# A state-space scan kernel: who carries the wait for a buffer's former sums, and when the second chunk's conv rows may start

## The chip, the cores and the metric

One core of one Trainium2 chip runs the whole program in one launch. Its engines are PE (TensorE: matmul; PEld is its weight load), DVE (VectorE), ACT (ScalarE), POOL (GpSimd) and SP (SyncE, which issues the DMAs here). Each has its own stream of instructions, in order; they meet through semaphores. The metric is the device time in microseconds (us); the time before is 6586.43, the median of three runs (6583.84 to 6587.49).

## The reference

Four layers on an image tensor of 4 x 96 x 64 x 64, fp32. Layer 0 is a selective scan in four directions with an MLP behind it, layer 1 a smaller scan, layer 2 a Fourier mixer and a quantized MLP, layer 3 a linear attention and a quantized MLP. The change touches layer 0 alone. Cut to what matters:

```python
# b = 4 images, L = 64*64, 192 inner channels d, 16 states n, 4 directions k
xz = t_ln @ in_proj_w.T + in_proj_b
xi, z = split(xz)
xi = silu(depthwise_conv_3x3(xi) + conv_b)
xs = the pixels of xi by rows, by columns, and both reversed      # [b, k, d, L]
x_dbl = einsum('bkdl,kcd->bkcl', xs, x_proj_w)                    # dts_r (6), Bs (16), Cs (16)
dt = softplus(einsum('bkrl,kdr->bkdl', dts_r, dt_projs_w) + dt_projs_b)
for each l:
    h = h * exp(dt[l] * A) + dt[l] * B[l] * x[l]                  # h: [b, k, d, n]
    y[l] = sum over n of h * C[l]
y = y + Ds * xs, the four directions are summed
out = (layernorm(y) * silu(z)) @ out_proj_w.T
```

## The kernel before, in words

**Steps and units.** The scan of layer 0 is cut into 64 steps: 4 images b, 4 directions k (in the order 0, 1, 3, 2), 4 chunks of 1024 pixels. A step has 24 units, 1536 in all. A unit is a tile of 128 partitions (32 channels x 4 states) by 1024 pixels; its index i is made of j (3 groups of channels), q (4 groups of states) and p (2 halves of the group), in the order j, q, p.

**One unit** goes through five coroutines:
- `sources` (L1498): POOL writes w = u * bb, with u = dt * x and bb = B loaded so that rows are repeated. The tile w comes from a ring of six buffers (`WB = 6`, L1356), so unit i takes the buffer of unit i - 6.
- `decays` (L1477): ACT writes h = exp(dt * A) into one of two PSUM tiles. The turn of decay i begins when the product of unit i - 2 is done; first a column of the old h is copied into `state`, which the same unit of the next chunk starts from.
- `recurs` (L1509): DVE runs the scan in place in h, with h and w as inputs; then, as its next instruction, the C product: w = h * cc, over the same w. A scan waits for ACT's h and POOL's w.
- `side` (L1535): for every twelfth unit the scan writes w, and POOL forms the product; 128 units go this way.
- `gathers` (L1544): PE adds the products of two units over the states with the matrix sel4 into the PSUM tile py, 32 rows at a time; `collects` (L1601) has ACT copy py to the sum Y.

**Waits.** The semaphores are set by the framework, which tracks who has read and written each tile. POOL's writing of w in unit i waits for PE's sums of unit i - 6, the last readers of that buffer. The C product writes the same tile, and in the program before most of these products wait for those sums on PE as well, besides the scan just ahead on DVE. [...]

**Chunks.** `preludes` (L1374) prepares a step: it loads xi, forms the 38 columns of x_proj on PE, stores B and C, forms delta (PE; Abs, Relu, Exp, Ln on ACT; an addition and a multiplication by x on POOL) and stores delta and delta * x to a DRAM tile dd. `loads_du` and `loads_bc` bring u, dt, bb and cc back with rows repeated. For the first step delta is formed in three pieces; when the last of them has its Ln, the event "begun" (L1422) is posted.

**The front of image 0.** `front(0)` (L456) normalizes and projects the image, then runs the 3 x 3 conv in 12 row blocks of 8 image rows: `conv(part, q)` (L560). Part 0 has 128 of the channels with q from 0 to 7; part 1 has the other 64, two halves of the image at once, with q from 0 to 3. A block is nine matmuls with diagonal weights into a PSUM bank (`bm`), or, if it is `early` (L568), nine multiply-adds on DVE (`taps`, L404); then Silu on ACT, a store to xi_d by SP, and a transposing copy to xt on POOL. Chunk 0 needs the blocks (0,0), (0,1), (1,0), (1,1); chunk 1 needs (0,2), (0,3), (1,2), (1,3). The blocks in `order` run ahead of the scan; the others, `rest_` (L613), in two workers beside it. [...]a Silu in the scan phase has a table load on each side. When all blocks are through, SP stores the transposed image for the directions 1 and 3.

**What sets the order.** The coroutines are driven by `Work` (L111 on), which keeps an estimated time for each engine and always advances the coroutine whose next instruction could start first (`choose`, L162). So the order on each engine is fixed when the program is built. A wait on an event such as "begun" holds a coroutine back in this planning; on the chip there are only the engines' streams and the semaphores. The layers behind the scan run as further coroutines (`others`, L1625) between the units, and for the last image after them.

Of the kernel before, what the change touches and what calls it, by code (L numbers as in the profile page):

```python
# [13 lines left out]
ALU = mybir.AluOpType  # L14
# [31 lines left out]
def size(x):  # L46
    return x.free_size() if hasattr(x, "free_size") else x[:].free_size()


def on(engine, *events, banks=0, took=0.7, table=None, unit=None):  # L50


    return engine, events, banks, took, table, unit
# [9 lines left out]
class Work:  # L63
# [40 lines left out]
    def post(self, *key, stored=False):  # L104
        self.events[key] = self.me.stored if stored else self.me.end
# [25 lines left out]
    def drop(self, *tiles):  # L131
        for t in tiles:
            self.free[self.held.pop(id(t))] = self.me.end
# [83 lines left out]
def tile_hybrid(ctx: ExitStack, tc: tile.TileContext, I: dict, out: bass.AP):  # L217
# [5 lines left out]
    def mm(o, lhsT, rhs, **kw):  # L223
        n = size(o)
        each = 0.97e-3 if rhs.dtype == E5M2 else 0.93e-3 if size(lhsT) <= 64 else 1.9e-3
        wk_.spend("pe", max(n * each, 0.3 if n > 4 else 0.2) + 0.02, 0.3)
        return nc.tensor.matmul(o, lhsT=lhsT, rhs=rhs, **kw)  # L227
# [5 lines left out]
    def act(o, i, func, **kw):  # L233

        want = TABLES.get(func, func if func in OTHER else None)
        if want is not None and want != wk_.table:
            wk_.spend("act", 1.28)
            if func in TABLES:
                nc.scalar.preload_act_table_set(want)
            wk_.table = want  # L240
        wk_.spend("act", 0.2 + size(o) * 0.87e-3)
        return nc.scalar.activation(o, i, func, **kw)  # L242
# [25 lines left out]
    ve, po_ = Side(nc.vector, "dve", on_vector), Side(nc.gpsimd, "pool", on_pool)  # L268
# [37 lines left out]
    def load_const(name, shape, src=None):  # L306
        t = const.tile(shape, F32, name=name)
        nc.sync.dma_start(t, I[src or name])
        return t
# [5 lines left out]
    sel4 = load_const("sel4", [128, 32])  # L315
# [7 lines left out]
    def V(name, rows=128, j=0, n=1):  # L323
        c, w = _COL[name]
        assert j + n <= w
        return vec[0:rows, c + j : c + j + n]
# [77 lines left out]
    def taps(acc, xp, row, w):  # L404

        o = acc.rearrange("p (h w) -> p h w", w=WW)
        for k in range(9):
            kh, kw = divmod(k, 3)
            v = xp[:, row + kh : row + kh + 8, kw : kw + 64]
            if k % 3 == 0:  # L410
                yield on("dve")
            if k == 0:
                ve.tensor_scalar(o, v, w[:, 0:1], None, ALU.mult)
            else:
                ve.scalar_tensor_tensor(o, v, w[:, k : k + 1], o, ALU.mult, ALU.add)
# [9 lines left out]
    def wt(pool, rows, name, t, cols=HC, dt=F32):  # L425
        name = f"{name}_{t}"
        return pool.tile([rows, cols] if isinstance(cols, int) else [rows, *cols], dt, tag=name, name=name)
# [28 lines left out]
    def front(b):  # L456
# [4 lines left out]
        ahead_ = b == 0  # L461
# [98 lines left out]
        def conv(part, q):  # L560
            dg, xt, xp = dgs[part], xts[part], (xp01, xp2)[part]

            def job(t):
                xi = wt(ck, 128, "xi", t)
                if b == 0 and q >= 2:
                    yield on(None, ("begun",))
                near = [("xp", b, v) for v in {q % 4, (q + 1) % 4, max(q - 1, 0) % 4, *((3,) if part and q == 0 else ())}]
                early = ahead_ and (part, q) in ((0, 0), (0, 1), (1, 0))  # L568
                (pc,) = yield on("dve" if early else "pe", *near, banks=1)
                if early:  # L570
                    yield from taps(pc, xp, 8 * q, V("cw", j=9 * part, n=9))
                for k in () if early else range(9):
                    kh, kw = divmod(k, 3)
                    r = 8 * q + kh
                    mm(
                        pc.rearrange("p (h w) -> p h w", w=WW), lhsT=dg[:, k, :],
                        rhs=xp[:, r : r + 8, kw : kw + 64], start=(k == 0), stop=(k == 8),
                    )
                    if k in (2, 5):
                        yield on("pe")  # L580
                if (part, q) == (1, 1):
                    post("ez")
                yield on("act", took=0.7, table=AF.Silu)
                act(xi, pc, AF.Silu, bias=V("cb", j=part))
                drop(pc)
                yield on("sp")
                if part == 0:
                    put(xi_d[b][0, q, 0:128], xi)
                else:
                    for h in range(2):  # L590
                        put(xi_d[b][0, q + 4 * h, 128:192], xi[64 * h : 64 * h + 64])
                post("rows", b, part, q, stored=True)
                yield on("pool")
                po_.tensor_copy(
                    xt[:, :, 8 * q : 8 * q + 8], xi.rearrange("p (h w) -> p w h", w=WW)
                )

            return job

        order = [(0, 0), (0, 1), (1, 0), (1, 1)] if ahead_ else []  # L600
# [9 lines left out]
        if not ahead_:  # L610
            stc, (xtp, ck) = pools(bg("f2"), bg("f2w"))
            xts = [xtp.tile([128, 64, rows], F32, name=f"xt{rows}") for rows in (64, 32)]
        rest_ = [(p, q) for p in (1, 0) for q in range(8 - 4 * p) if (p, q) not in order]  # L613
        yield from par([conv(p, q) for p, q in rest_], 2)
        yield on("sp")
        v = xi_d[b][1, :, 0:128, :].rearrange("g d t -> d g t")
# [3 lines left out]
        v = xi_d[b][1, :, 128:192, :].rearrange("g d (w h) -> d g w h", h=HH)  # L620
# [733 lines left out]
    NS_ = len(steps)  # L1354
    NU = UNITS * NS_
    WB, DB, RB, SIDE = 6, 3, 5, 12  # L1356
    made, weights = {}, {}
    live = dict(h={}, w={}, state={}, Y=None, py=None)
    fg = {}

# [148 lines left out]
    def recurs():  # L1509
        for i in range(NU):  # L1510
            g, j, q, p, n = place(i)
            b, k, s, c = steps[g]
            need = [("h", i), ("src", i), ("cc", 4 * g + q)]
            if s:
                need.append(("st", i - UNITS))
            yield on("dve", *need)
            wk_.pace = i, max(wk_.me.start, wk_.at["dve"])
            if i % UNITS == 0 and s == 0:
                live["state"][b, k] = fg["ck"].tile([128, 24], F32, tag="state", name="state")
            h, w, state = live["h"][i], live["w"][i], live["state"][b, k]  # L1520
            first = 0.0 if s == 0 else state[:, n : n + 1]
            o = w if i % SIDE == SIDE - 1 else h
            if k >= 2:
                ve.tensor_tensor_scan(o[:, ::-1], h[:, ::-1], w[:, ::-1], first, ALU.mult, ALU.add)
            else:
                ve.tensor_tensor_scan(o, h, w, first, ALU.mult, ALU.add)
            if o is w:
                post("scan", i)
                live["h"][i] = o
                continue  # L1530
            yield on("dve")
            ve.tensor_mul(w, h, made[g]["cc", q])
            post("C", i)
# [10 lines left out]
    def gathers():  # L1544

        for i in range(1, NU, 2):
            g, j, q, p, n = place(i)
            block = 3 * g + j
            k = steps[g][1]
            if q == 0:  # L1550
                yield on("pe", *([("py", block - 1)] if block else []), *([] if k else [("xj", block)]))
                py = live["py"] = fg["py"].tile([128, HC], F32, tag="py", name="py")
                if k:
                    o = py.rearrange("p (r w) -> p r w", w=16) if k % 2 else py
                    mm(o, lhsT=eye128, rhs=y_part(block), start=True, stop=False)
                else:
                    mm(py, lhsT=diagD[:, j], rhs=live["xj"], start=True, stop=False)
                    post("xjf", block)
            yield on("pe", ("C", i))
            for p in range(2):  # L1560
                w = live["w"].pop(i - 1 + p)
                for f in range(2):
                    r = p * 64 + f * 32
                    o = live["py"][r : r + 32]
                    if k % 2:
                        v = w.rearrange("p (w c f h) -> p f c h w", c=4, f=2, h=8)[:, f]
                        o = o.rearrange("p (c h w) -> p c h w", c=4, h=8)
                    else:
                        v = w[:, f * HC : (f + 1) * HC]
                    mm(o, lhsT=sel4, rhs=v, start=False, stop=(q == 3))  # L1570
            post("g", i // 2)

    def y_part(block):
# [59 lines left out]
    with tc.manual_schedule():  # L1633
# [5 lines left out]
        first = wk_.add(setup()), wk_.add(front(0))  # L1639
# [199 lines left out]
```

## Time and profile before

| | us |
|---|---|
| median of three runs | 6586.43 |
| the profiled execution, its own time | 6589.22 |
| span of that execution | 6587.4 |
| first scan of the first chunk starts at | 93.23 |
| first scan of the second chunk starts at | 204.28 |
| last sums of the scan end near | 6026 |

The page of the profile gives shares of busy time, the groups of instructions, and the waits. "Idle before" in a group is the time in which the engine stood just ahead of its instructions, with what ended most of it. The group of the scans in the page's part 5, for comparison:

```profile
L254 DVE TENSOR_TENSOR_SCAN h<-h,state,w 128x1024 f32<-128x1024 f32 x1056 | 2480.8, 2349 | 195.4 <-ACT h L242 111.7
...
L254 POOL TENSOR_TENSOR w<-u,bb 128x1024 f32<-128x1024 f32 x1536 | 3608.7, 2373 | 881.5 <-PE py L227 800.3
L227 PE MATMUL py<-w,sel 128*32 128x512 f32 x6144 | 1796.2, 933 | 496.5 <-DVE w L254 332.1
L242 ACT ACTIVATE h<-dt,negA 128x1024 f32<-128x1024 f32 x1536 | 1727.7, 1125 | 394.8 <-DVE w L254 292.1
```

L227, L242, L254, L231, L275 and L279 are the lines of helpers that all instructions of a kind go through (matmul, activation, DVE and POOL operations, ACT copy, load and store), so groups are told apart by tile names: h, w, cc, u, bb, py as above; xi and xp of the conv; dtu for delta. A matmul of 512 fp32 columns shows as two records on PE.

### The profile page before, as it was taken

The numbers are of one execution on the slowest core, as the hardware profiler recorded it, in microseconds if no ns is written. First come the engines' busy times: TensorE is split into PE (matmuls) and PEld (weight loads), VectorE is DVE, ScalarE is ACT, GpSimd is POOL, SyncE is SP. The second block draws the span as 40 slices with busy tenths as digits, with TensorE's granted clock in tenths as the row PEclk, the third lists the DMA queues.
The fourth block names the chain that finished last, engine by engine and source line by source line (L and its number), as shares of the span: only waits on it lengthen the run. The fifth ranks groups of instructions, "written<-read, shape, count | busy, mean of one in ns | idle before, by whom it ended". The sixth has DMA issues, their size and how long they took to land. (4 is left out here: it accounts for less than half of the span.)

```text
span 6587.4 us, 55972 instructions
## 1 busy us (share of the span) xinstructions
PE 5261.5 (80%) x15770; PEld 1657.9 (25%) x15770; DVE 5753.2 (87%) x3863; ACT 4317.5 (66%) x6528; POOL 4740.2 (72%) x2152
## 2 busy tenths in 40 slices
PE   7578897977867988777778888777778888877788
PEld 2122221222211332212211332212211232212273
DVE  5799999999988999999889999999989999996613
ACT  5466766666766557877666567876666567885636
POOL 4678787877798777877698777887699777883000
PEclk8689898988978999879778999888779999888778
DMA  4665556565565684555455685555555685552451
GB/s 149 202 185 184 177 166 204 172 211 178 162 196 170 225 269 152 185 183 182 156 183 180 211 280 168 169 192 178 163 181 176 200 291 179 162 185 74 151 159 34
DMA packets 532512, 1189.24 MB, mean 181 GB/s; under 512 B 90286, under 2 KB 163579, under 8 KB 532188
## 3 DMA queue, kind: packets, MB, share of 16 engines
q1 hardware_dynamic: 532200, 1185.66, 57.7%
q8 instruction: 125, 2.05, 0.1%
q14 instruction: 187, 1.53, 0.1%
HBM read 937.80 MB, written 247.63 MB: 180 GB/s over the span
## 5 line engine op out<-in xcount | busy, mean ns | idle before, releaser
L254 POOL TENSOR_TENSOR w<-u,bb 128x1024 f32<-128x1024 f32 x1536 | 3608.7, 2373 | 881.5 <-PE py L227 800.3
L254 DVE TENSOR_TENSOR_SCAN h<-h,state,w 128x1024 f32<-128x1024 f32 x1056 | 2480.8, 2349 | 195.4 <-ACT h L242 111.7
L227 PE MATMUL py<-w,sel 128*32 128x512 f32 x6144 | 1796.2, 933 | 496.5 <-DVE w L254 332.1
L242 ACT ACTIVATE h<-dt,negA 128x1024 f32<-128x1024 f32 x1536 | 1727.7, 1125 | 394.8 <-DVE w L254 292.1
L254 DVE TENSOR_TENSOR w<-h,cc 128x1024 f32<-128x1024 f32 x1408 | 1721.7, 1223 | 108.5 <-DVE h L254 2.3
L254 DVE TENSOR_TENSOR_SCAN h<-h,w 128x1024 f32<-128x1024 f32 x352 | 805.7, 2289 | 100.8 <-DMA u<-dd 34.5
L231 ACT COPY state<-h 128x1 f32<-128x1 f32 x1056 | 166.4, 158 | 785.1 <-DVE w L254 783.4
L227 PEld LDWEIGHTS py<-w,sel 128*32 128x32 f32 x6144 | 185.1, 114 | 1535.7 <-DVE w L254 861.6
L254 POOL TENSOR_TENSOR w<-w,cc 128x1024 f32<-128x1024 f32 x128 | 301.6, 2357 | 150.7 <-ACT state L231 105.4
L227 PE MATMUL bm<-xp,dg 128*128 128x512 f32 x792 | 375.8, 617 | 0.0
L227 PE MATMUL bm<-xi,xw 128*128 128x512 f32 x378 | 224.9, 742 | 101.9 <-DMA xi<-xi_d 92.7
L254 POOL TENSOR_TENSOR dtu<-dtu 128x1536 f32<-128x1536 f32 (+1 forms) x66 | 221.7, 3358 | 103.0 <-ACT dtu L242 55.4
L242 ACT ACTIVATE dtu<-bm 128x512 f32<-128x512 f32 x382 | 208.4, 600 | 62.2 <-PE bm L227 61.2
L227 PE MATMUL bm<-xd,dtw 64*128 64x512 f32 x382 | 223.8, 670 | 21.1 <-ACT xd L242 11.3
L254 DVE TENSOR_TENSOR_SCAN w<-h,state,w 128x1024 f32<-128x1024 f32 x96 | 224.8, 2342 | 5.2 <-ACT h L242 5.0
L254 POOL TENSOR_TENSOR dtu<-dtu,xi 128x1536 f32<-128x1536 f32 (+1 forms) x66 | 221.5, 3356 | 3.9
L227 PEld LDWEIGHTS bm<-xp,dg 128*128 128x128 f32 x792 | 147.7, 195 | 290.3 <-issue 282.9
L227 PE MATMUL bm<-big,dg 96*96 96x512 f32 x432 | 208.5, 625 | 11.4 <-ACT u L242 7.6
L227 PE MATMUL py<-Y,eye 128*128 128x512 f32 x288 | 166.2, 660 | 44.4 <-ACT Y L231 35.6
L227 PE MATMUL bm<-x,cent 96*96 96x512 f32 x284 | 159.4, 657 | 31.8 <-DMA x<-in_x 16.4
L242 ACT ACTIVATE bm<-bm,eps 96x512 f32<-96x512 f32 (+1 forms) x211 | 136.9, 649 | 64.9 <-PE bm L227 64.3
L242 ACT ACT_TABLE_LOAD x121 | 155.2, 1283 | 8.6 <-PE bm L227 4.6
(325 smaller groups left out, 6953.8 us busy)
## 6 DMA issues: line engine op xcount, KB each, us to landing
u<-dd SPq DMA_DIRECT2D x384, 512.0 KB
dt<-dd SPq DMA_DIRECT2D x384, 512.0 KB
bb<-bc SPq DMA_DIRECT2D x256, 512.0 KB
cc<-bc SPq DMA_DIRECT2D x256, 512.0 KB
dd<-dtu SPq DMA_DIRECT2D x252, 384.0 KB
xi<-xi_d SPq DMA_DIRECT2D x256, 192.0 KB
f_d<-fo SPq DMA_DIRECT2D x64, 384.0 KB
a<-f_d SPq DMA_DIRECT2D x64, 384.0 KB
```

The costliest lines, as they stand in the source:

```text
L227: return nc.tensor.matmul(o, lhsT=lhsT, rhs=rhs, **kw)
L231: return nc.scalar.copy(o, i, **kw)
L242: return nc.scalar.activation(o, i, func, **kw)
L254: return f(o, *a, **kw)
```

## The change

Two edits. First, each scan from unit 6 on is given an explicit dependency on the last sum that read the former occupant of its w buffer (its name is kept in `summed` when `gathers` emits it). The framework then counts that wait as met when it comes to the C product behind the scan. Second, in the front of image 0 the blocks with q = 2 and 3 no longer wait for "begun"; (0,2) is added to the early ones, which DVE computes; and the remaining blocks run by q, both parts, ahead of q = 4 and on.

```diff
@@ conv(part, q), in front(b)
-                if b == 0 and q >= 2:
+                if b == 0 and q >= 4:
                     yield on(None, ("begun",))
...
-                early = ahead_ and (part, q) in ((0, 0), (0, 1), (1, 0))
+                early = ahead_ and (part, q) in ((0, 0), (0, 1), (1, 0), (0, 2))
...
-        rest_ = [(p, q) for p in (1, 0) for q in range(8 - 4 * p) if (p, q) not in order]
+        rest_ = [(p, q) for q in range(2, 4) for p in (1, 0)] if ahead_ else []
+        rest_ += [(p, q) for p in (1, 0) for q in range(8 - 4 * p) if (p, q) not in order + rest_]
@@ tile_hybrid
-    made, weights = {}, {}
+    made, weights, summed = {}, {}, {}
+    anti = mybir.DependencyInfo(mybir.DependencyClass.Sync, mybir.DependencyReason.ANTI)
@@ recurs
             if k >= 2:
-                ve.tensor_tensor_scan(o[:, ::-1], h[:, ::-1], w[:, ::-1], first, ALU.mult, ALU.add)
+                it = ve.tensor_tensor_scan(o[:, ::-1], h[:, ::-1], w[:, ::-1], first, ALU.mult, ALU.add)
             else:
-                ve.tensor_tensor_scan(o, h, w, first, ALU.mult, ALU.add)
+                it = ve.tensor_tensor_scan(o, h, w, first, ALU.mult, ALU.add)
+            if i >= WB:
+
+                tc.add_manual_dep(it.ins, summed.pop(i - WB), anti, reason="sums of what lay in w")
@@ gathers
-                    mm(o, lhsT=sel4, rhs=v, start=False, stop=(q == 3))
+                    summed[i - 1 + p] = mm(o, lhsT=sel4, rhs=v, start=False, stop=(q == 3)).ins.name
```

The scans, products and sums themselves, their operands and their number stay as they are; of the conv blocks one moves from PE to DVE.

## The prediction

> **What bounds the kernel now.** I read the page's busy shares first, then its groups of instructions, then the waits of DVE, then the timeline around the two places that the change touches. Page, parts 1 and 5 (busy us, mean ns | idle before them):
>
> ```profile
> PE 5261.5 (80%) x15770; PEld 1657.9 (25%) x15770; DVE 5753.2 (87%) x3863; ACT 4317.5 (66%) x6528; POOL 4740.2 (72%) x2152
> ...
> L254 DVE TENSOR_TENSOR w<-h,cc 128x1024 f32<-128x1024 f32 x1408 | 1721.7, 1223 | 108.5 <-DVE h L254 2.3
> ```
>
> By stretch (the windows view: span, busy us of PE, PEld, DVE, ACT, POOL, granted clock, DMA share, GB/s):
>
> ```profile
> 93.00:181.00 88.00, 79.74 (x228) 28.72 (x229) 80.21 (x46) 57.56 (x79) 64.52 (x32) 0.93 0.55 190
> 181.00:204.00 23.00, 8.36 (x22) 3.08 (x20) 0.00 (x0) 5.88 (x7) 11.02 (x5) 0.79 0.62 169
> ...
> 260.00:6026.00 5766.00, 4633.87 (x13744) 1356.89 (x13742) 5400.63 (x3391) 3892.57 (x5814) 4615.38 (x2078) 0.88 0.60 188
> 6026.00:6587.00 561.00, 445.36 (x1558) 237.93 (x1554) 202.02 (x343) 296.55 (x525) 0.21 (x2) 0.82 0.37 109
> ```
>
> DVE works 94% of the scan phase (5400.6 of 5766); the last 561 us hold none of the 1536 units. In 181 to 204 DVE does nothing at all. The timeline of DVE (start, length, what, idle before):
>
> ```profile
> 113.89 2.29 DVE L254 TENSOR_TENSOR_SCAN h<-h,w 128x1024 f32<-128x1024 f32 x1
> 116.21 1.22 DVE L254 TENSOR_TENSOR w<-h,cc 128x1024 f32<-128x1024 f32 x1
> 117.35 2.29 DVE L254 TENSOR_TENSOR_SCAN h<-h,w 128x1024 f32<-128x1024 f32 x1
> 119.73 1.23 DVE L254 TENSOR_TENSOR w<-h,cc 128x1024 f32<-128x1024 f32 x1
> ...
> 176.68 2.28 DVE L254 TENSOR_TENSOR_SCAN w<-h,w 128x1024 f32<-128x1024 f32 x1
> 204.28 2.36 DVE L254 TENSOR_TENSOR_SCAN h<-h,state,w 128x1024 f32<-128x1024 f32 x1 [25.33 <-ACT state L231]
> ```
>
> Unit 5's product (116.21) follows its scan (113.89 + 2.29) at once, by 0.03 us; unit 6's (119.73) comes 0.09 after. Unit 6 is the first whose w buffer had a former occupant. The 25.33 us are the step to the second chunk. SP's queue shows what they wait for:
>
> ```profile
> 188.99 4.22 SPq L279 DMA_DIRECT2D dd<-dtu  x4
> 193.31 1.87 SPq L279 DMA_DIRECT2D xi_d<-xi  x1
> 195.28 1.71 SPq L275 DMA_DIRECT2D u<-dd  x1
> ```
>
> The chunk's delta is stored from 188.99 on and loaded back from 195.28 on, with 204.28 as the outcome.
>
> [...]
>
> **Part 1, the products.** In the order of the program before, such a product has a record that waits for DVE (its own scan), sometimes for a DMA too, and the instruction itself waits for PE. [...] I sorted all pairs of a scan and the product straight behind it by the gap between them: 795 with the record for the scan alone have a median of 104 ns; 175 with a DMA in the record too have 91; 203 whose product carries the wait for its scan itself, most with no record at all, have 34. The rest of the 1408 follow another instruction and overlap it by 80. After the change no product waits for PE, and the scans do not either, since POOL's writing of w, which they wait for, had waited for the same sums. So 795 x 70 ns + 175 x 57 ns = 55.7 + 10.0 = 65.6 us of DVE's time go. No data is waited for less; no instruction is added.
>
> How much of it arrives at the end? I followed each instruction from 6026 back to 93 to whichever of its predecessors came last (the semaphores' counts tell which). 553 of the 970 pairs lie on that chain (472 and 81): 472 x 70 + 81 x 57 = 37.7 us. It is an upper bound if every other leg keeps its length: those run over PE 1081, ACT 755, POOL 643 and SP 326 us, where DVE's gain only lengthens a wait such as these (who waited, for whom: total us, times, longest):
>
> ```profile
> DVE h L254 <- ACT h L242: 125.9, 124, 8.8
> DVE h L254 <- ACT state L231: 79.2, 29, 25.3
> DVE h L254 <- POOL w L254: 53.9, 41, 2.7
> ```
>
> A decay may start once the product two units back has ended, so each of these 194 waits bypasses at least one pair. Where DVE's legs get shorter, PE's and POOL's come up beside them; I take a fifth off for that, by judgement: **30 us**. Ends: 15 (most legs have a rival close by) and 65.6 (all).
>
> **Part 2, the front.** On all engines the order changes in the first 200 or so instructions alone; behind them the same instructions follow each other. What moves, engine by engine, with durations of before:
> - DVE: nine tap instructions of row block (0,2), 0.75 + 6.30 us, behind those that end at 58.74. They end near 65.8; the first scan is at 93.23, inside an idle time of 34.50. Free; without that cover 7.
> - ACT: two Silu of (0,2) and (1,2), 0.69 each, with four table loads of 1.28, come between the first delta and the first decay. Six conv matmuls of 0.9 (5.4 us) stand on PE before the second delta matmul. ACT then reaches the first decay near 89.4; that waits for the load of dt until 92.02. Slack 2.6 us; the first scan stays at 93.2.
> - POOL: the second and third deltas (2 x 1.27 each) stand behind w(1) and w(3) instead of ahead of w(0) and behind w(1). Scan 3 comes near 105.6 instead of 106.96.
> - The rows of chunk 2: the last that it needs is through Silu near 120.1 ((1,3)) instead of 144.78 ((0,3)); its xi loads start near 123.5 instead of 145.23. On PE its first product stands behind the sums of unit 7 instead of unit 15: 132.9 instead of 157.44. Delta's Ln, now behind decay 19, is at 161 instead of 180.37, POOL's two passes of 3.43 end at 169.6 instead of 188.96, SP stores from 169.6 instead of 188.99. The store of row block (0,7), moved ahead of the loads, waits for ACT's Silu near 177.1, so u is issued at 177.6 instead of 195.28: 17.7 earlier.
> - Delta's Exp now lies between decays 17 and 18: about 2.2 us of new stall at scan 18, inside the slack below.
> - DVE ends chunk 1 near 179.4 (178.96 before) and starts chunk 2 at 204.28 - 17.7 = 186.5. Some 7 us of stall remain: delta is still late, not the rows.
>
> What is late next are stalls of 4.21 at 234.32 and 8.77 at 251.66, behind SP's stores of the transposed rows and its parameter loads; that queue starts 18 to 20 us earlier too. So **18 us** hold. Ends: 10 (a row, a bank or that store later than reckoned) and 26 (the whole stall).
>
> **Sum.** 30 + 18 = 48. The profiled execution took 6589.2 (span 6587.4), so 6541 there; the median of the three runs lies 2.8 below it: **6538**.
>
> **Rivals.**
> - Only the front arrives, the products' gain goes into waits for ACT and POOL: 6586.4 - 18 = 6568. For it: 417 of 970 pairs are already off the chain. Against it: DVE is at 94%.
> - The front gives nothing (chunk 2 still at 204): 6556. For it: SP's queue is long[...]. Against it: everything ahead of u is at least 17 us earlier.
> - All 65.6 and 18 arrive: 6503. It needs ACT, POOL and PE to follow; they mostly wait for DVE (page: POOL idles 800 for sums, ACT as long for products).
> - Both vanish, the end within 13 us: 6580.
> - Slower: PE's granted clock. PE is busy 80% and on the chain for 1081 us[...]. Each per cent costs 10.8 us; it decides from 48 / 10.8 = 4.4% on, 0.836. At 0.82 it costs 71: 6609. Against it: in the scan phase the clock was 0.88 with PE 80% busy, and 0.65 where PE idled (204 to 260).
> - That the wait moves to the scan and costs there what it cost here: 6568. But in the built order the scans wait for Activation and POOL alone.
>
> **Chances.** Forecast 0.62 (its own range 6518 to 6556), only the front 0.12 (the scan carrying the wait counts here), front without effect 0.09, all of it 0.10, both vanish 0.04, slower 0.03. The range 6508 to 6568 takes in the rivals on both sides but for those three. A change of 0.2% (13 us) is about what can be told from none here: faster 0.93, same 0.04, slower 0.03.
>
> **What would show it.** Idle before the products falls from 108.5 to about 43 us (970 of them at 34 instead of 104 or 91); DVE's records of separate waits fall by 850 or so. Scan 24 starts near 186, with about 7 us of idle. Scans' idle for ACT and POOL grows by 20 to 35 us in total: that is the part of 65.6 that does not arrive. I am wrong if products keep 90 ns, if scan 24 is beyond 195, or if those waits grow by 60.

## The result and the profile after

| | before | after |
|---|---|---|
| median of six runs each, us | 6587.15 (6583.84 to 6590.83) | 6529.03 (6511.34 to 6541.84) |
| ratio, 95% interval | | 0.9911 [0.9897, 0.9926] |
| profiled execution, span, us | 6587.4 | 6525.4 |
| mean granted clock of PE | 0.874 | 0.875 |

The change takes off 58 us (the interval of the ratio gives 49 to 68) where 48 were forecast. The page of the changed kernel, parts 1 and 5, in the columns of before:

```profile
PE 5217.8 (80%) x15752; PEld 1648.8 (25%) x15752; DVE 5763.1 (88%) x3872; ACT 4316.9 (66%) x6530; POOL 4739.1 (73%) x2152
...
L254 DVE TENSOR_TENSOR_SCAN h<-h,state,w 128x1024 f32<-128x1024 f32 x1056 | 2481.0, 2349 | 197.5 <-ACT h L242 123.1
...
L254 DVE TENSOR_TENSOR w<-h,cc 128x1024 f32<-128x1024 f32 x1408 | 1721.4, 1223 | 40.4
```

The product takes 1223 ns in both. What went is the time ahead of it, 108.5 us before and 40.4 now. Unit 6, whose product came 0.09 us behind its scan before, now has it 0.03 behind (113.38 + 2.29):

```profile
113.38 2.29 DVE L254 TENSOR_TENSOR_SCAN h<-h,w 128x1024 f32<-128x1024 f32 x1
115.70 1.22 DVE L254 TENSOR_TENSOR w<-h,cc 128x1024 f32<-128x1024 f32 x1
```

All 1173 products that stand straight behind their scan now start 33 to 35 ns after its end; before, only 203 did. DVE's separate records of waits fell from 2892 to 2035.

The windows view of the changed kernel (span, busy us of PE, PEld, DVE, ACT, POOL, granted clock, DMA share, GB/s), by the stretches of before:

```profile
181.00:204.00 23.00, 8.61 (x22) 1.35 (x22) 20.29 (x12) 9.22 (x14) 22.73 (x11) 0.57 0.87 252
260.00:5960.00 5700.00, 4584.67 (x13709) 1351.21 (x13710) 5380.30 (x3376) 3877.65 (x5792) 4592.98 (x2066) 0.88 0.61 190
```

In 181 to 204, where DVE did nothing before, it now works for 20.29 of 23 us. The end of the scan phase comes at 5962 instead of 6023 (the end of the last scan), and what lies behind it is as long as before: from the start of the last scan to the end of the span, 565.9 us against 566.6. So all the gain is made inside the scan phase.

Where in that phase? I took the start of the same scan in both traces; the difference is the lead of the changed kernel (us):

| scan | 0 | 18 | 24 | 72 | 360 | 648 | 936 | 1224 | 1535 |
|---|---|---|---|---|---|---|---|---|---|
| lead | 2.7 | 2.7 | 20.8 | 19.2 | 27.7 | 38.1 | 47.3 | 61.5 | 61.3 |

A step of 18 at scan 24, the first of the second chunk, and then a slope of some 3 us per hundred scans: two effects that can be told apart by eye. The 2.7 us at the first scan are no part of either (see the front, below). DVE's timeline of the changed kernel has what is left of the step (start, length, what, idle before):

```profile
67.16 0.75 DVE L254 TENSOR_SCALAR bm<-xp,vec 128x512 f32<-128x512 f32 x1 [9.55 <-ACT z L242]
...
90.57 2.30 DVE L254 TENSOR_TENSOR_SCAN h<-h,w 128x1024 f32<-128x1024 f32 x1 [16.32 <-POOL xt L254]
...
156.32 2.30 DVE L254 TENSOR_TENSOR_SCAN h<-h,w 128x1024 f32<-128x1024 f32 x1 [1.96 <-ACT state L231]
...
183.50 2.36 DVE L254 TENSOR_TENSOR_SCAN h<-h,state,w 128x1024 f32<-128x1024 f32 x1 [7.58 <-ACT state L231]
...
213.10 2.36 DVE L254 TENSOR_TENSOR_SCAN h<-h,state,w 128x1024 f32<-128x1024 f32 x1 [4.79 <-ACT state L231]
...
230.16 2.36 DVE L254 TENSOR_TENSOR_SCAN h<-h,state,w 128x1024 f32<-128x1024 f32 x1 [8.49 <-ACT h L242]
```

The stall of 25.33 us at scan 24 has shrunk to 7.58. The taps at 67.16 stand in idle time that DVE had anyway. The last two lines are the stalls of 4.21 and 8.77 us of before, at the same scans.

### The profile page after: what moved, and what is told of

It reads as the page before. It is cut to its first block, busy times and chain, and to the rows that moved or that the text cites. A ratio compares the mean times of both kernels' runs of the same rounds, so it can differ in the third digit from the quotient of the medians.

```text
span 6525.4 us, 55088 instructions
## 1 busy us (share of the span) xinstructions
PE 5217.8 (80%) x15752; PEld 1648.8 (25%) x15752; DVE 5763.1 (88%) x3872; ACT 4316.9 (66%) x6530; POOL 4739.1 (73%) x2152
## 4 chain that ended last, share of the span: by engine, by line
DVE 21%; PE 18%; issue 9%; ACT 8%; POOL 7%; DMA 4%; SPq 1%; DVEq 0%; POOLq 0%; ACTq 0%
DVE h L254 15%; PE bm L227 11%; POOL w L254 5%; PE py L227 4%; DVE w L254 4%; PE be L227 3%; ACT h L242 3%; DMA xi<-xi_d 1%; ACT h L231 1%; ACT dtu L242 1%; SPq L275 1%; ACT bm L242 1%; POOL dt L254 1%; POOL a L254 1%; DVE a L254 0%
## 5 line engine op out<-in xcount | busy, mean ns | idle before, releaser
L227 PE MATMUL py<-w,sel 128*32 128x512 f32 x6144 | 1774.4, 933 | 476.2 <-DVE w L254 318.8
L254 DVE TENSOR_TENSOR w<-h,cc 128x1024 f32<-128x1024 f32 x1408 | 1721.4, 1223 | 40.4
L231 ACT COPY state<-h 128x1 f32<-128x1 f32 x1056 | 166.0, 157 | 746.3 <-DVE w L254 744.8
```

Source lines behind the costliest of these rows:

```text
L231: return nc.scalar.copy(o, i, **kw)
L254: return f(o, *a, **kw)
```

## The experiments

Theory: each edit works by itself. The first one brings what the chain of last predecessors says, that is the 553 pairs on it and nothing of the other 417; the second brings a fixed lead at scan 24. Rivals: the first edit's gain goes into waits for ACT and POOL; the front's lead is lost later; a part of an edit would have done as well.

### 1. Each edit alone

The first edit alone is the diff of the change without its lines of `conv` and `rest_`; the front alone is those lines. The first edit, shortened:

```diff
@@ recurs
...
-                ve.tensor_tensor_scan(o, h, w, first, ALU.mult, ALU.add)
+                it = ve.tensor_tensor_scan(o, h, w, first, ALU.mult, ALU.add)
+            if i >= WB:
+                tc.add_manual_dep(it.ins, summed[i - WB], anti, reason="sums of what lay in w")
...
@@ gathers
-                    mm(o, lhsT=sel4, rhs=v, start=False, stop=(q == 3))
+                    summed[i - 1 + p] = mm(o, lhsT=sel4, rhs=v, start=False, stop=(q == 3)).ins.name
```

The first edit alone:

> The first edit alone: every scan from unit 6 on carries the dependency, the front is as before. If the two edits add up and the front is worth what scan 24 shows in the profile (20.8 us earlier), this one has the other 37 of the 58 us: about 6550. If the products' gain is eaten by waits for ACT and POOL and the front made the rest of the difference: 6568 or more. Idle before the products about 43 us in either case.

The front alone:

> The second edit alone: front as in the changed kernel, products and scans as before. If the lead at scan 24 is kept to the end, 20 to 22 us less than before: about 6566. If the lead melts away among the later waits: 6575 to 6587. Idle before the products stays near 108 us.

| | median, us | ratio to before | scan 24's lead | last scan's lead |
|---|---|---|---|---|
| before, same chip, 35 runs | 6588.41 | | | |
| first edit alone, 5 runs | 6552.93 | 0.9948 [0.9933, 0.9963] | 2.2 | 37.3 |
| front alone, 22 runs | 6571.90 | 0.9974 [0.9966, 0.9982] | 16.9 | 17.6 |

The first edit brings 35 us (24 to 44), as a slope over the whole scan phase; the front brings 17 us (12 to 22), all of them by scan 24, and keeps them to the end. That is what the two shapes in the table of leads say. Their sum, 52, is within the interval of the 58 measured for both, so no effect of one edit on the other has to be assumed. The 20 to 22 expected of the front were too many: I had taken them from the 20.8 of lead at scan 24 of the changed kernel, and alone the front has 16.9 there.

### 2. The first edit, for the units on the chain and for the others

From the trace of before I had followed each instruction back to its last predecessor. Of the 970 pairs whose gap should shrink, 553 lie on that chain and 417 do not. Two kernels have the first edit for one of the two sets each, by a mask over the unit's index. Against the first edit alone:

```diff
+    CARRIED = int("...", 16)
...
-            if i >= WB:
+            if i >= WB and CARRIED >> i & 1:
                 tc.add_manual_dep(it.ins, summed[i - WB], anti, reason="sums of what lay in w")
```

On the chain:

> The first edit for 553 units alone, those whose scan and product lie on the chain followed back through the profile of the kernel before. If the chain says which products matter, this has nearly the whole gain of the first edit: 35 to 38 us, about 6550. If all 970 products are worth the same, 57% of it: about 21 us, 6566.

Off the chain:

> The first edit for the other 417 units, whose pairs lie off that chain. If the chain decides: 0 to 6 us, 6581 to 6587. If all products are worth the same, 43%: about 16 us, 6571.

| | pairs | median, us | ratio to before |
|---|---|---|---|
| on the chain, 6 runs | 553 | 6550.32 | 0.9945 [0.9928, 0.9961] |
| off the chain, 14 runs | 417 | 6586.48 | 1.0004 [0.9994, 1.0014] |

This is the sharpest result of the study. 553 pairs give 38 us (26 to 47 by the interval) where the bound was 37.7, and 417 give nothing (between 4 us faster and 9 slower). The 21 and 16 us that they would have brought if all products were worth the same lie outside. The waits view shows where the gain of the others went. The kernel with the pairs on the chain (who waited, for whom: total us, times, longest):

```profile
DVE h L254 <- ACT h L242: 124.0, 117, 9.7
DVE h L254 <- ACT state L231: 79.3, 29, 25.2
DVE h L254 <- POOL w L254: 53.8, 45, 2.7
```

And the one with the others:

```profile
DVE h L254 <- ACT h L242: 140.4, 137, 8.6
DVE h L254 <- ACT state L231: 86.5, 32, 25.1
DVE h L254 <- POOL w L254: 57.8, 43, 2.7
```

Before, these three sum to 259.0. With the pairs on the chain they sum to 257.1: DVE's idle time ahead of the products fell by 39.2 (108.5 to 69.3), and none of it came back as such a wait. With the others they sum to 284.7: the products' idle time fell by 28.5 (108.5 to 80.0), and 25.7 of it came back. Two executions of one kernel (the last two rows of the table in section 4) differ by 9 in this sum, 245.0 and 253.9, so "none" holds to within that; the 25.7 are well above it. Scans that wait for a decay or for POOL anyway waited longer there once DVE got to them sooner. What "off the chain" means is seen here in the scans' own waits.

### 3. Which part of the front's edit it is

It has three: (0,2) on DVE, the hold on "begun" lifted for q = 2 and 3, and the new order of the blocks. I left out each in turn, and tried the order alone, on the kernel before. What is read is the start of scan 24 in the profile.

```diff
@@ lifting the hold
-                if b == 0 and q >= 2:
+                if b == 0 and q >= 4:
@@ (0,2) on DVE
-                early = ahead_ and (part, q) in ((0, 0), (0, 1), (1, 0))
+                early = ahead_ and (part, q) in ((0, 0), (0, 1), (1, 0), (0, 2))
@@ the new order
-        rest_ = [(p, q) for p in (1, 0) for q in range(8 - 4 * p) if (p, q) not in order]
+        rest_ = [(p, q) for q in range(2, 4) for p in (1, 0)] if ahead_ else []
+        rest_ += [(p, q) for p in (1, 0) for q in range(8 - 4 * p) if (p, q) not in order + rest_]
```

Without (0,2) on DVE:

> The kernel before with two of the three edits of the front: rows (0,2), (1,2), (0,3), (1,3) come first and in chunks, and only (0,4) and later wait for the deltas of the first step; (0,2) stays on TensorE. Theory (the lead comes from the rows being let through before the deltas are done): scan 24 starts 13 to 19 us earlier than in the kernel before (204.3), near the 16.9 of all three edits together, and TensorE's nine more matmuls (some 15 us of it in that stretch) cost at most 4 of these. Rival (a row on VectorE in its idle time is what brings it): scan 24 starts at most 8 us earlier. One look: the place of scan 24 is read, the total says little.

Without the new order:

> The kernel before with two of the three edits of the front: row (0,2) on VectorE, and the rows of the second chunk let through before the deltas; the order of the rows that are left is as before, (1,2) and (1,3) before (0,2) and on. Theory (a row of the second chunk must be off TensorE while the input product still runs, since TensorE's rows come one in some 10 us once the scans run): scan 24 starts 8 to 20 us earlier than in the kernel before (204.3), near the 16.9 of all three edits, since two rows in hand at a time take (1,2), (1,3), (0,2) almost together. Rival (the order is needed too): 0 to 5 us. One look, at the place of scan 24.

Without lifting the hold:

> The kernel before with two of the three edits of the front: row (0,2) on VectorE and the new order; rows from (0,2) on still wait for the deltas of the first step, so its taps come when the scans have begun, 7.3 us of them between scans. Theory (the row has to be off TensorE while VectorE is idle, ahead of the first scan): scan 24 starts at most 8 us earlier than in the kernel before (204.3), and some scan before it has a stretch of taps ahead of it. Rival (it is enough that TensorE has one row less to do): 13 to 19 us earlier. One look, at the place of scan 24.

The order alone:

> The kernel before with one of the three edits of the front, the order of the rows that are left; rows from (0,2) on still wait for the deltas of the first step. Theory (the wait is what held the second chunk): most of the lead stays away, scan 24 starts 0 to 7 us earlier than in the kernel before (204.3); something comes of the order alone, since the row (1,2) no longer stands behind (0,4) and later. Rival (the order is what brings it): 13 to 19 us earlier. One look, at the place of scan 24.

| edits of the front | fourth Silu of the second chunk at | lead at scan 24, us |
|---|---|---|
| none (before) | 144.1 | |
| all three | 118.6 | 16.9 |
| without (0,2) on DVE | 139.4 | 1.3 |
| without the new order | 134.1 | 4.9 |
| without lifting the hold | 142.9 | -1.9 |
| the order alone | 143.8 | 0.4 |

Two of my four theories fell. Letting the blocks through with (0,2) left on PE brings 1.3, not 13 to 19, and without the new order 4.9 are left, not 8 to 20; the other two held. These are single profiles, good to some 2 us, but no pair of the edits comes near what all three do. The second chunk needs four blocks, and the lead is large only where the fourth of them has its Silu early. The ACT timeline shows these four, first with all three parts:

```profile
81.41 0.69 ACT L242 ACTIVATE xi<-bm,vec 128x512 f32<-128x512 f32 x1
87.06 0.69 ACT L242 ACTIVATE xi<-bm,vec 128x512 f32<-128x512 f32 x1
111.36 0.69 ACT L242 ACTIVATE xi<-bm,vec 128x512 f32<-128x512 f32 x1
118.58 0.69 ACT L242 ACTIVATE xi<-bm,vec 128x512 f32<-128x512 f32 x1
```

then without (0,2) on DVE:

```profile
101.39 1.26 ACT L242 ACTIVATE xi<-bm,vec 128x512 f32<-128x512 f32 x2
134.63 0.69 ACT L242 ACTIVATE xi<-bm,vec 128x512 f32<-128x512 f32 x1
139.44 0.69 ACT L242 ACTIVATE xi<-bm,vec 128x512 f32<-128x512 f32 x1
```

In the trace of before each of the five Silu between 93 and 165 us has a table load of 1.28 us on either side (108.41 and 110.72 around the one at 109.71). Of the four Silu of the second chunk the first two come ahead of the first scan (at 92) with all three parts, and behind the third delta without one of them (at 101.4, 101.6 and 108.8). PE's timeline has the conv matmuls, 18 records to a block. With all three parts the second of PE's blocks ends with the first of these lines, and the next begins with the other:

```profile
99.33 3.79 PE L227 MATMUL bm<-xp,dg 128*128 128x512 f32 x6
104.05 2.84 PE L227 MATMUL bm<-xp,dg 128*128 128x512 f32 x6
```

and without (0,2) on DVE:

```profile
92.00 2.84 PE L227 MATMUL bm<-xp,dg 128*128 128x512 f32 x6
112.83 7.55 PE L227 MATMUL bm<-xp,dg 128*128 128x512 f32 x12
```

PE is through with two blocks even earlier there. But with all three parts DVE has made a third, so one is left from 104.05 on; without (0,2) on DVE two are left, and they begin only at 112.83, 18 us after the second has ended. The fourth is through at 118.6 in one case and at 139.4 in the other. Without the new order and without lifting the hold the taps of (0,2) moreover stood among the scans, from 116.69 and from 99.40 on. So all three parts were needed to have two blocks through before the first scan. Whether PE's start at 112.83 comes from the three PSUM banks, from the later Silu or from the planner's estimate was not told apart.

### 4. What is late next, and a version beyond the change

I took the stall left at scan 24 (7.58) for the delta of the second step, made and stored in one piece, and the stalls at 213.10 and 230.16 for SP's queue, where 15 loads of parameters for the preparation of later layers stand ahead of loads of dt. Three kernels, from the changed one: the second step's delta in three pieces; that, and the preparation behind the fourth step's loads of u and dt; that, with the second step's instead of the fourth's. The diff is of the third; the second has ("du", 23), the first leaves `others` alone.

```diff
-            for j0, j1 in ((0, 1), (1, 2), (2, 3)) if g == 0 else ((0, 3),):
+            for j0, j1 in ((0, 1), (1, 2), (2, 3)) if g <= 1 else ((0, 3),):
@@ others
-        yield on(None, ("front", 0))
+        yield on(None, ("front", 0), ("du", 11))
         yield from prepare()
```

Three pieces:

> The changed kernel, with the deltas of the second step made and stored in three pieces of one j each, as those of the first step are, where it makes them in one. Theory (what is late at scan 24 after the change is the u and dt of step 1, whose store waits for all three j): the 7.6 us of idle time at scan 24 go, the scan starts 5 to 8 us earlier than in the changed kernel, and the end comes 3 to 8 us earlier. Rival (the decays' table loads and twelve more issues in the queue of SP give it back, or the stalls at 213.1 and 230.2 grow): end within 3 us of the changed kernel, at a ratio of 0.991 to the kernel before. Under the theory the ratio is 0.990.

With the preparation behind the fourth step's loads:

> As v_split, and the preparation of the weights of the later layers is started only after the u and dt of the fourth step are issued, so that its 15 loads no longer stand in the queue of SP ahead of the dt that the scans at 213.1 and 230.2 wait for (4.8 and 8.5 us in the changed kernel). Theory: those two stalls shrink to under 3 us each, the lead over the changed kernel at scan 48 is 12 to 20 us, and the ratio to the kernel before is 0.988 to 0.989. Rival (the stalls are of the xi and bc of step 2, that is of the end of the front, and not of the queue): lead at scan 48 as v_split's, 5 to 8 us; or the work that is put off is missed later and takes the lead back, end within 3 us of the changed kernel.

With the preparation behind the second step's loads:

> The changed kernel with the deltas of the second step in three pieces, and the preparation of the weights of the later layers started once the u and dt of the second step are issued (in the kernel with both edits it was the fourth). Theory (the put-off work was missed later, since all that follows it shifted by some 130 us and 57 us of it came to lie behind the last scan; a shift of some 30 us leaves the later packing as it is): the stall of 15.1 us at scan 230.1 of the kernel with three pieces alone goes, the lead over that kernel at scan 48 is 10 to 25 us, at least half of it is left at the last scan, and the ratio to the kernel before is 0.985 to 0.988. Rival (what is taken from the work beside the scans is given back behind them, whatever the shift): the lead at scan 48 is lost by the last scan, ratio 0.988 or above.

The same kernel once more:

> The kernel with the deltas of the second step in three pieces and the weights prepared after the second step's loads, once more, since its ratio (0.9896, 0.9880 to 0.9913) does not tell it from the changed kernel (0.9911, 0.9897 to 0.9926). Its place in one profile was 23.7 us ahead of the changed kernel's at the end of the span. Theory (that is a real lead): ratio to the kernel before 0.987 to 0.989. Rival (the time between runs of one kernel differs by more than this lead, and one profile overstates it): 0.990 or above.

| | median, us | ratio to before, same chip | scan 48 at | last scan at | from there to the end |
|---|---|---|---|---|---|
| changed kernel | 6529.03 | 0.9911 [0.9897, 0.9926] | 292.5 | 5959.6 | 565.9 |
| three pieces | 6513.37 | 0.9884 [0.9870, 0.9898] | 288.6 | 5944.9 | 566.0 |
| and preparation behind step 4's loads | 6605.61 | 1.0027 [1.0019, 1.0034] | 262.1 | 5980.9 | 622.9 |
| and preparation behind step 2's loads | 6508.66 | 0.9896 [0.9880, 0.9913] | 271.7 | 5936.6 | 565.1 |
| the last one again | 6513.37 | 0.9890 [0.9871, 0.9909] | 270.2 | 5949.4 | 561.5 |

The three pieces remove the stall at scan 24: from the first scan to that one it is 85.1 us instead of 92.9. Here is DVE's timeline of that kernel:

```profile
179.47 2.36 DVE L254 TENSOR_TENSOR_SCAN h<-h,state,w 128x1024 f32<-128x1024 f32 x1 [0.52 <-ACT h L242]
...
230.08 2.36 DVE L254 TENSOR_TENSOR_SCAN h<-h,state,w 128x1024 f32<-128x1024 f32 x1 [15.07 <-ACT h L242]
```

The two later stalls have become one of 15.07 us, and SP's timeline shows what it waits for:

```profile
223.01 0.42 SPq L275 DMA_DIRECT2D sc<-in_l_sc  x1
223.54 0.58 SPq L275 DMA_DIRECT2D dt<-dd  x1
```

The load of dt comes straight behind the last of the parameter loads. With the preparation put off, the same load goes out some 20 us earlier:

```profile
202.94 0.59 SPq L275 DMA_DIRECT2D dt<-dd  x1
```

That is the kernel that waits for step 2's loads, and the stall is gone there: scan 48 starts 16.9 us earlier than with the three pieces alone. So the reading is right for the stall at 230. For the one at 213.10 it was not. These lines of the changed kernel, of SP and then of ACT, show what stood ahead of it:

```profile
179.08 21.22 SPq L279 DMA_DIRECT2D xi_d<-xt  x18
200.35 2.04 SPq L275 DMA_DIRECT2D xi<-xi_d  x4
...
211.11 0.69 ACT L242 ACTIVATE xd<-bm,vec 128x512 f32<-128x512 f32 x1 [8.51 <-PE bm L227]
```

The loads of xi for the third step stand behind the 18 stores of the transposed image, PE's product with xw, at 206.44, waits for them, and ACT's copy of that product stands ahead of the decay of the late scan. The parameter loads begin only at 205.35, behind these. In the kernel with three pieces the loads of xi are issued at 177.72, ahead of the stores, and the stall at 213 is gone without any postponement.

What the postponement is worth is another matter. The kernel with the longest postponement is 30 us ahead of the changed one at scan 48 and 15 us slower than the kernel before at the end. It is the clearest case here of an early gain that is paid back: its lead over the changed kernel falls from 37.7 at scan 72 to -21.3 at the last scan, and behind the last scan lie 622.9 us instead of 565.9. Work of the later layers that filled gaps beside the scans was begun later and came to lie behind them: from the start of the last scan to the end PE is busy 503.7 us there, 450.3 in the changed kernel. That fits the longer tail, but not the 59 us lost between scan 72 and the last: DVE's scans wait 310 us for decays, states and POOL there, 261 in the changed kernel, and why was not looked into. With the shorter postponement the tail stays as it is. But of the 16.9 us only 8.3 were left at the last scan of one profile, and the other profile of the same kernel has its last scan 12.9 us later. That is as much as the lead. In both postponements the gain at scan 48 came (30.4 and 16.9 us, where 12 to 20 and 10 to 25 were expected), and the gain at the end did not: ratios of 1.0027 and 0.9896 are the rivals', not the theories'.

The ratios of the three pieces and of the shorter postponement, 0.9884 to 0.9896, are all below the changed kernel's 0.9911, which is 10 to 18 us. Their intervals overlap with its own, and they were measured beside other runs of before. For the three pieces 3 to 8 us were expected; where more would come from was not asked. So a version some 10 us faster than the change is likely, not shown; postponing the preparation showed no gain over the three pieces.

## Why the prediction was right

- **The gaps.** 970 pairs at 104 or 91 ns going to 34, DVE saving 65.6 us: the products' idle time fell by 68.1 and ended at 40.4 (about 43 said); separate records fell by 857 (850 said). The scans did not take over the wait: with the first edit alone no wait ahead of them grew but for ACT and POOL, and the scan behind a product still overlaps it by some 83 ns (median, before and after). That rival is out. The records' own times in the trace of before show where the 104 ns lie: the record that waits for the scan ends 59 ns (median of the 795) after the scan, later than the 34 at which a product that carries the wait has begun, and the product starts 45 after the record. So these products begin only behind their record, and that ends behind the scan. Why a wait in a record takes longer than a carried one was not shown. In 53 pairs of the changed kernel the record waits for a DMA alone and ends 2.3 us (median) ahead of the scan's end; their products start at 34 or 35, so there a record as such cost nothing. How much of the 45 belongs to the wait for PE, which the same products carried, is not told apart.
- **What a carried wait costs.** In the trace of before 35 other instructions (writing hs) stand straight behind a scan without waiting for it, and start some 90 ns (median) before its end; the product that carries the wait starts 34 after. By these numbers the carried wait is the cheaper form, not a free one.
- **How much of it arrives.** Here a term was probably mis-sized. No run speaks against the 37.7 us from the chain; the fifth that I took off "by judgement", since PE's and POOL's legs might come up beside it, was not seen. The pairs on the chain gave 38 with no growth of waits beyond the 9 us that two executions differ by. A fifth is less than that, and the 30 us lie within the intervals too (26 to 47, and 24 to 44 for the first edit alone), so that the discount was wrong is likely, not shown. The growth of 20 to 35 us in the scans' waits was forecast rightly in size (29.0 with the first edit alone: 144.7 + 84.6 + 58.7 against 259.0), but it is the share of the pairs off the chain, 25.7 of it, and had been counted when these were left out. If so, taking the fifth off charged for it twice.
- **The front.** 18 forecast, 17 measured alone. The steps in the changed kernel: last Silu of the second chunk at 116.1 (120.1 said), the product with xw at 127.5 (132.9), Ln at 157.4 (161), store of delta at 166.0 (169.6), u issued at 175.07 (177.6), scan 24 at 183.5 (186.5) with 7.58 of stall (7). All are some 2.5 to 5.4 early. 2.7 of that is the first scan, at 90.57 where I had left it at 93.2: ACT's decay for it, which waits for the load of dt, starts at 89.36 instead of 92.02. The front alone puts that scan at 92.4, and two executions of one further kernel put it at 93.7 and 91.5, so this difference is no effect of the edit that one profile could show.
- **The taps** were forecast at 58.7 to 65.8, and came at 67.16, after 9.55 us of waiting for ACT's writing of the input rows. They were free all the same, since the first scan waited 16.32 more. I had looked at DVE's idle time but not at when the taps' input is there.
- **The small stall** at scan 18, 2.2 us, is there with 1.96. The later stalls of 4.21 and 8.77 are there with 4.79 and 8.49, 21 us earlier, so the lead held across them, as said.
- **The slower rival**, a lower clock of PE: 0.875 against 0.874. It did not come.
- **The sum.** 48 said, 58 measured, 52 as the sum of the two edits measured alone. Of the ten missing, some 5 are the first edit (35 instead of 30), 1 less is the front, and 6 are the difference between 52 and 58, within the intervals.

What was right by less than it looked is the front. The forecast treated its three parts as one path and did not ask what each is worth; asked afterwards, I got two of the four answers wrong.

## What to carry to other kernels

Follow each instruction back to its last predecessor, and count the shortened gaps that lie on that chain. Here that sum arrived as far as the runs can tell, and the waits that grew belonged to the gaps off the chain, so a discount for the same waits on top has no ground in these runs. In these traces DVE's wait for the scan just ahead left 34 ns where the product carried it and 91 to 104 where a record ahead held it, so if an instruction has two waits, see whether an earlier instruction of the same engine can take the other. A stall that is removed by putting work off must be looked at behind the last iteration as well as at the stall.

## What was not expected of the hardware

- A record that waits for the scan alone left 104 ns between scan and product, one that waits for a DMA too 91, against 34 for the carried wait. The difference lies in the record, which ends 59 ns after the scan in the first case and 46 in the second; the product starts 45 after the record in both. Why the record with more to wait for ends sooner is open.
- One kernel's runs differ more than its first six say: before, six runs lie within 7 us (6583.84 to 6590.83), and the 35 runs beside the first experiments within 35 (6568.39 to 6603.01). Two profiles of the same kernel differ by 2.2 us at the first scan, by 1.5 at scan 48 and by 12.9 at the last. By this one pair, a lead at an early scan can be read from one profile to some 2 us, and one at the end to no better than 13.
